# A linear-attention and mixture-of-experts layer on one core: feeding the routing block by block and moving slot lists, shared experts and routed experts between rounds

## The chip, the cores and the metric

The kernel runs on one NeuronCore of a Trainium2 chip. A core has TensorE (PE in the profile, with its weight loads as PEld), VectorE (DVE), ScalarE (ACT), GpSimd (POOL) and SyncE (SP), each with its own instruction stream in order, and 16 DMA engines that serve the queues of SP, ACT and POOL. The metric is the device time of one execution in microseconds (us). All data are float32.

## The reference

There are 4096 tokens (4 sequences of 1024) of 256 channels. The layer normalizes x and adds two branches to it: linear attention with 16 heads of 16 channels and four memory banks, and a mixture of 8 routed experts (two for each token, hidden size 176) with a shared expert of hidden size 352.

```python
xn = _layernorm(x, axis=-1)
x = x + _L0_attn_ref(xn, ...) + _L0_ffn_ref(xn, ...)
...
# attention
sq = elu1(q)
out_coarse = ...   # sq on the summed memory banks
out_fine = (outs * w).sum(0)          # sq on each bank, weighted
gprob = jax.nn.sigmoid(jax.nn.relu(coarse_repr @ eg_w1.T + eg_b1) @ eg_w2.T + eg_b2)
memory_output = exp_prob * out_fine + (1.0 - exp_prob) * out_coarse
local_output = causal_linear_attention(q, k, v)
gate = jax.nn.sigmoid(memory_gate).reshape(1, NH, 1, 1)
output = gate * memory_output + (1.0 - gate) * local_output
return output.transpose(0, 2, 1, 3).reshape(B, S, H) @ w_o.T
...
# experts
scores = jax.nn.softmax(logits, axis=-1)
topk_w, topk_idx = jax.lax.top_k(scores, K)
topk_w = topk_w / (jnp.sum(topk_w, axis=-1, keepdims=True) + 1e-20)
g = jax.nn.silu(jnp.einsum('th,efh->tef', x, w_gate)) * jnp.einsum('th,efh->tef', x, w_up)
expert_out = jnp.einsum('tef,ehf->teh', g, w_down)
y = jnp.einsum('te,teh->th', cw, expert_out).reshape(b, s, h)
y = y + _swiglu_mlp(x, sw_gate, sw_up, sw_down).reshape(b, s, h)
```

## The kernel before

A tile is 128 tokens, a block is 4 tiles; there are 32 tiles (`NTT`) and 8 blocks (`NBLK`). The order of the work is written out by hand: the Python program issues the instructions in the order in which each engine runs them, and waits between engines follow from the data and from the rotating buffers.

**Prelude.** SP's queue loads the eight blocks of x (`load_x`) and then all weights and constants except wvg, wq and wk, which are on ACT's queue. The string `ahead` gives the order of steps for each block: S (`statistics`: mean and variance of a row on DVE, then the power -0.5 on POOL for one or two blocks at once), N (`normalize`: half the tiles on DVE, half on ACT, in place, then SP's queue stores the block to `xns` in DRAM), T (`transpose_x`) and V (`values`: PE makes the values and the router's logits; ACT copies the values into the buffer that held x, and POOL sets their ones and zeros). The values overwrite the normalized x, so these writes wait for the store to `xns`. `masks`, `memories`, `gates`, `living` and `route` (the first and second largest logit, for half of the tokens) stand between them. After the prelude SP copies x to `sums` in DRAM, where the experts' results are added.

**Start.** The sorting of the tokens by expert (`route(1)`, `sort`, `weights`, `owners`; on DVE) runs beside the first query, key and shared-expert projections, among them the shared expert of block 0.

**Rounds.** Round n works on tile n in attention, with parts of tiles n-1 and n-2 (`attention_round`): scores, masks, memory, local part, the transposition back, the state update, and the output projection of tile n-2 (for tiles below 24). `quad`, four PSUM banks, holds the scores and then the memory products. All other PSUM results take turns in a pool of four banks (`bank`, tag r). Beside the attention round lie up to three further streams, which `mix` merges by the share of each stream's weight that is done:

- `lists`, in rounds 0 to 3 (`first_round` = 4): the slot lists that say which token stands in which slot of which expert. For each of 22 batches of three columns DVE makes one-hots (L540, L544; in buffers of the experts' weights), ACT and POOL weigh them (L557, L560), and PE adds them up in one bank, "found" (L568), which stays taken until the lists are done. `inverted` then gives `islot` and `wslot`.
- `beside`: shared expert of block 1 over rounds 0 to 3, then from round 4 for each block 2 to 7 over four rounds the keys of that block, the queries of the next one and (up to block 6) its shared expert (`projections`). The shared expert's hidden values stay in buffers with the tag h (2 x `NF` = 6 of 2 KB) until the output of their block.
- `side`, rounds 4 to 29: the routed experts, 71 tiles of slots (`NST`). `expert_turn` fetches rows of `xns` (an indirect DMA on POOL's queue, L1006) and weights (SP's queue), and transposes; `expert_hidden` (L1052, L1057 to L1059), `expert_out` (L1065, L1069), and `put`, an indirect DMA that adds the rows to `sums` (L1074). Each put waits for the one before it. A planner gives each round as many units as fill it up to a common level, at most 1.5 times the mean.

```python
    work = experts()
    share = [weight(rounds[n]) + weight(beside[n]) for n in range(first_round, last_round)]
    level = max(share)
    cap = 1.5 * weight(work) / len(share)
```

**Tail.** Round 30 has the shared expert of block 7. Then the outputs of tiles 24 to 31, which were held, run with rounds 31 to 33; `sums` is read back (L942, L978), added (L966, L992) and stored.

Of the kernel before, what the change touches and what calls it, by code (L numbers as in the profile page):

```python
# [8 lines left out]
FP = mybir.dt.float32  # L9
# [5 lines left out]
P = 128  # L15
# [7 lines left out]
def linear_attention_moe_kernel(  # L23
# [76 lines left out]
    def load_x(blk):  # L100

        wide = big.tile([P, NT, VW], FP, tag="tok", name=f"x_{blk}")
        xb = wide[:, :, :H]
        nc.sync.dma_start(
            xb, x[blk * TB : (blk + 1) * TB, :].rearrange("(n p) h -> p n h", p=P)
        )
        st["x", blk] = xb
        st["wide", blk] = wide

    for blk in range(NBLK):  # L110
        load_x(blk)

    def load_weight(w, name, engine=nc.sync):
        t = const.tile([P, NC, w.shape[1]], FP, tag=name, name=name)
        engine.dma_start(t, w.rearrange("(k p) c -> p k c", p=P))
        return t

    wvg = load_weight(w_vg, "wvg", nc.scalar)
    wq = load_weight(w_q, "wq", nc.scalar)
    wk = load_weight(w_k, "wk", nc.scalar)  # L120
    raw = const.tile([P, NC, NMN, D1], FP, tag="raw", name="raw")
    nc.sync.dma_start(
        raw[:, :, 1:NMN, :], memories.rearrange("(c p) m k -> p c m k", p=P)
    )
    gate = const.tile([P, NH], FP, tag="gate", name="gate")
    nc.sync.dma_start(gate, memory_gate.to_broadcast([P, NH]))
    b2 = const.tile([P, 1], FP, tag="b2", name="b2")
    nc.sync.dma_start(b2, eg_b2.to_broadcast([P, 1]))
    w1 = load_weight(eg_w1, "w1")
    b1 = const.tile([P, HID], FP, tag="b1", name="b1")  # L130
    nc.sync.dma_start(b1, eg_b1.rearrange("h o -> o h").to_broadcast([P, HID]))
    w2 = const.tile([P, HID], FP, tag="w2", name="w2")
    nc.sync.dma_start(w2, eg_w2.rearrange("h o -> o h").to_broadcast([P, HID]))
    wo = load_weight(w_o, "wo")
    wg = load_weight(w_gate[:, FR:], "wg")
    wu = load_weight(w_up[:, FR:], "wu")
    wd = const.tile([P, NF, H], FP, tag="wd", name="wd")
    full = FS // P
    nc.sync.dma_start(
        wd[:, :full, :],  # L140
        w_down[FR : FR + full * P, :].rearrange("(f p) h -> p f h", p=P),
    )
    if full < NF:
        nc.sync.dma_start(wd[: FS - full * P, full, :], w_down[FR + full * P :, :])

# [10 lines left out]
    nc.gpsimd.memset(ones, 1.0)  # L156
    neghalf = const.tile([P, 2 * NT], FP, tag="neghalf", name="neghalf")
    nc.gpsimd.memset(neghalf, -0.5)
# [46 lines left out]

    pick = tmp.tile([P, 2, NTT, E], FP, tag="h", name="pick", bufs=2 * NF)
    picks, pick = pick, [pick[:, r] for r in range(2)]
    lgs = tmp.tile([P, 2, NTT, E], FP, tag="h", name="lgs", bufs=2 * NF)
    lgs, gatew = lgs[:, 0], lgs[:, 1]

    more = tmp.tile([P, 2, E, NTT], FP, tag="h", name="more", bufs=2 * NF)[:, 0]
    nc.gpsimd.memset(more, 1.0)
# [16 lines left out]

    def sigmoid(v):  # L230

        nc.scalar.activation(v, v, AF.Exp, scale=-1.0)
        nc.vector.tensor_scalar(v, v, 1.0, None, ALU.add)
        nc.vector.reciprocal(v, v)

    def masks():
# [5 lines left out]
        for c in range(NC):  # L242
            nc.vector.tensor_copy(own_s[:, c], own[:, :, None].to_broadcast([P, HC, D1]))

    def gates_of_heads():
        nc.vector.tensor_scalar(gate, gate, -80.0, None, ALU.max)
        sigmoid(gate)
        nc.vector.tensor_scalar(ungate, gate, -1.0, 1.0, ALU.mult, ALU.add)
        nc.vector.tensor_copy(
            gates.rearrange("p (h k) -> p h k", k=HD), gate[:, :, None].to_broadcast([P, NH, HD])  # L250
        )
        nc.vector.tensor_scalar(b2, b2, 0.5, None, ALU.mult)
# [39 lines left out]

    def statistics(blk):

        xb = st["x", blk]
        if blk == 0 or blk % 2:
            st["mv"] = small.tile([P, 2, NT, 2], FP, tag="mv", name=f"mv_{blk}", bufs=3)
            st["rstd"] = small.tile([P, 2, NT], FP, tag="rstd", name=f"rstd_{blk}", bufs=3)
        mv, rstd = st["mv"], st["rstd"]
        at = (blk + 1) % 2 if blk else 0  # L300
        for i in range(NT):
            stats = small.tile([P, 6], FP, tag="stats", name=f"stats_{blk}_{i}")
            nc.vector.bn_stats(stats, xb[:, i, :])
            nc.vector.bn_aggr(mv[:, at, i, :], stats)
        st["norm", blk] = mv[:, at], rstd[:, at]
        if blk % 2 == 0 or blk == NBLK - 1:
            n = at + 1
            some = rstd[:, :n].rearrange("p b i -> p (b i)")
            nc.vector.tensor_scalar(
                some, mv[:, :n, :, 1].rearrange("p b i -> p (b i)"), LN_EPS, None, ALU.add  # L310
            )
            nc.gpsimd.tensor_tensor(some, some, neghalf[:, : n * NT], ALU.pow)

    def normalize(blk):

        xb = st["x", blk]
        mv, rstd = st.pop(("norm", blk))
        shift = small.tile([P, NT], FP, tag="shift", name=f"shift_{blk}")
        nc.vector.scalar_tensor_tensor(
            shift, mv[:, :, 0], -1.0, rstd, ALU.mult, ALU.mult  # L320
        )
        xnT = io.tile([P, NC, TB], FP, tag="xnT", name=f"xnT_{blk}")
        st["xnT", blk] = xnT
        half = NT // 2
        for i in range(half, NT):
            nc.vector.tensor_scalar(
                xb[:, i, :], xb[:, i, :], mv[:, i, 0:1], rstd[:, i : i + 1],
                ALU.subtract, ALU.mult,
            )
        for i in range(half):  # L330
            nc.scalar.activation(
                xb[:, i, :], xb[:, i, :], AF.Identity,
                bias=shift[:, i : i + 1], scale=rstd[:, i : i + 1],
            )
        nc.sync.dma_start(
            xns[blk * TB : (blk + 1) * TB, :].rearrange("(n p) h -> p n h", p=P), xb
        )

    def transpose_x(blk, pair):
# [81 lines left out]
    def weights():  # L421
# [7 lines left out]
        two = st["two"]  # L429
        both = tmp.tile([P, 2, NTT, E], FP, tag="h", name="chosen", bufs=2 * NF)  # L430
        yield
# [497 lines left out]
    def shared_hidden(blk, f):  # L929
        n = min(P, FS - f * P)  # L930
        th, pu = st.pop(("th", blk, f))
        h = tmp.tile([P, TB], FP, tag="h", name=f"h_{blk}_{f}", bufs=2 * NF)
        nc.vector.scalar_tensor_tensor(h[:n], th[:n], 0.5, pu[:n], ALU.mult, ALU.mult)
        st["h", blk, f] = h
# [147 lines left out]

    first_round, last_round = 4, 30

# [53 lines left out]
    def projections(blk):  # L1138

        pairs = keys(blk) + (queries(blk + 1) if blk + 1 < NBLK else [])  # L1140
        pairs += shared(blk) if blk + 1 < NBLK else []
        units = [u for pair in pairs for u in pair]
        if blk % BPB == 0:
            b = blk // BPB
            at = units.index(pairs[3][1]) + 1
            units[at:at] = [(64, mean_queries, b)]
            at = units.index(pairs[6][0])
            units[at:at] = [(64, batch_weights, b)]
# [22 lines left out]
    def experts():  # L1171
        units = [(2000, lambda: None), (256, expert_turn, -2), (256, expert_turn, -1)]
        for j in range(NST + 1):
# [7 lines left out]
    def split(units, parts):  # L1181
# [14 lines left out]

    ahead = "S0 S1 masks N0 T0 S2 S3 N1 N2 V0 T1 T2 S4 memories V1 S5 N3 N4 V2 T3 T4 S6 gates V3 S7"
    ahead += " N5 N6 V4 living T5 T6 N7 V5 route V6 T7 V7"
    other = {
        "masks": masks, "memories": memories_by_group, "gates": gates_of_heads, "living": living,  # L1200
        "route": lambda: [None for _ in route(0)],
    }
    with tc.tile_pool(name="ps_v", bufs=2, space=bass.MemoryType.PSUM) as ps_v:
        for what in ahead.split():
            if what in other:
                other[what]()
                continue
            blk = int(what[1:])
            if what[0] == "S":
                statistics(blk)  # L1210
            elif what[0] == "N":
                normalize(blk)
            else:
                for pair in range(NT // 2):
                    (transpose_x if what[0] == "T" else values)(blk, pair)

# [22 lines left out]

    rounds = [attention_round(n) for n in range(NTT + 2)]  # L1240
    beside = [[u for pair in shared(1) for u in pair if u]] + [projections(blk) for blk in range(2, NBLK)]
    beside = [units for run_of in beside for units in split(run_of, NT)] + [[]] * (NT + 2)
    lists = []
# [20 lines left out]
    level = max(share)  # L1264
    cap = 1.5 * weight(work) / len(share)
    while sum(min(cap, max(0, level - s)) for s in share) < weight(work):
# [80 lines left out]
```

## Time and profile before

| | us |
|---|---|
| median of 3 runs (lowest, highest) | 720.52 (717.43, 724.11) |
| the profiled execution, its own time | 720.73 |
| its span, first to last instruction | 718.8 |
| PE busy in the span | 656.1 (91%) |
| DVE busy | 455.8 (63%) |
| POOL busy | 385.6 (54%) |
| ACT busy | 266.9 (37%) |

The profile comes from one execution. "Busy" of an engine is the time in which at least one of its instructions ran; matmuls are pipelined, so a busy PE isn't at its peak. A row of a timeline gives the start, the time taken, the engine, the line of the kernel, the operation, what it writes and reads, its size, how many instructions are merged, and in square brackets how long the engine stood idle before it and what ended that. A row of the windows view gives for a stretch of time the busy time of each engine with the number of instructions, the clock granted to PE (1.00 is full), the share of the DMA engines' time, and GB/s.

Rounds are found in the trace by their first matmuls, the scores (L691): round 0 starts at 88.7 us, round 4 at 165.2, round 26 at 583.4, round 30 at 671.7.

### The profile page before, as it was taken

Reading aid. Unit: us, or ns where it says so; the run is one execution under the profiler, and the core shown is the slowest. Engines: PE = TensorE matmul, PEld = TensorE weight load, DVE = VectorE, ACT = ScalarE, POOL = GpSimd, SP = SyncE. Lnnn points to the kernel's source line nnn. Section 1 sums busy time; section 2 is a strip of 40 time slices with the busy share of each in tenths; the row PEclk is TensorE's granted clock in tenths of the full one; section 3 lists DMA queues with packets and bytes.
Section 4 is the critical chain, followed back from the end, with each engine's and each line's share of the span. In section 5 each row is a group of like instructions: output and inputs, shape, how many; then the busy total and the mean of one; then the engine's idle time right before and its main releaser. Section 6 shows DMA issues by size and latency. Waiting matters only on the chain.

```text
span 718.8 us, 14242 instructions
## 1 busy us (share of the span) xinstructions
PE 656.1 (91%) x5084; PEld 468.4 (65%) x5084; DVE 455.8 (63%) x1193; ACT 266.9 (37%) x614; POOL 385.6 (54%) x436
## 2 busy tenths in 40 slices
PE   3699987888999999999999999999999987998987
PEld 2585465675676667766676766676767765665666
DVE  6544888886675656665756665657656654454764
ACT  3365443333433343334333442344333433243310
POOL 3210034455465566565664564646665777666576
PEclk9899988999999999999999999999999999699999
DMA  9556000014344444443444453535445676575285
GB/s 295 175 189 190 1 1 1 1 29 115 86 108 102 111 98 89 103 119 86 115 108 91 108 107 77 123 91 116 111 96 123 136 182 145 123 157 126 30 269 206
DMA packets 86466, 81.50 MB, mean 113 GB/s; under 512 B 7533, under 2 KB 83997, under 8 KB 86269
## 3 DMA queue, kind: packets, MB, share of 16 engines
q1 hardware_dynamic: 70797, 60.14, 29.1%
q0 software_dynamic: 13632, 18.62, 15.2%
q10 hardware_dynamic: 1968, 1.84, 0.7%
q8 instruction: 40, 0.66, 0.4%
q14 instruction: 29, 0.24, 0.1%
HBM read 62.62 MB, written 22.15 MB: 118 GB/s over the span
## 4 chain that ended last, share of the span: by engine, by line
PE 71%; DMA 9%; DVE 8%; POOL 4%; ACT 4%; issue 3%; SPq 0%; ACTq 0%; POOLq 0%; DVEq 0%
PE phe L1052 11%; PE pye L1065 7%; PE psu L921 6%; PE po L958 6%; PE pg L907 5%; DMA sums<-y,islot 4%; PE quad L691 4%; PE pn L717 4%; PE po L962 4%; PE quad L806 3%; PE pk L600 3%; PE pq L600 3%; PE pv L362 2%; PE pte L1039 2%; PE pte L1043 2%
## 5 line engine op out<-in xcount | busy, mean ns | idle before, releaser
L1074 POOL DMA_INDIRECT sums<-y,islot x71 | 113.3, 1595 | 80.0 <-DMA sums<-y,islot 28.4
L1052 PE MATMUL phe<-wgu,turned 128*128 128x352 f32 x276 | 99.5, 484 | 2.5 <-ACT turned L1045 1.2
L1058 DVE SCALAR_TENSOR_TENSOR hidden<-hidden,phe 128x176 f32<-128x176 f32 x71 | 23.8, 335 | 117.8 <-ACT hidden L1057 113.2
L698 DVE TENSOR_TENSOR sT<-quad,causal 128x512 f32<-128x512 f32 x128 | 80.6, 681 | 8.1 <-PE quad L691 7.8
L1006 POOL DMA_INDIRECT xg<-xns,islot x71 | 70.3, 990 | 19.7 <-issue 10.6
L1065 PE MATMUL pye<-wdn,turned 88*128 88x256 f32 x284 | 77.3, 395 | 1.8 <-issue 1.4
L828 POOL TENSOR_TENSOR cg<-coarse,gates 128x256 f32<-128x256 f32 x32 | 24.5, 767 | 98.0 <-DVE h L885 53.5
L1052 PEld LDWEIGHTS phe<-wgu,turned 128*128 128x128 f32 x276 | 49.5, 195 | 27.0 <-issue 8.3
L1065 PEld LDWEIGHTS pye<-wdn,turned 88*128 88x128 f32 x284 | 51.2, 194 | 15.3 <-issue 6.7
L1069 ACT ACTIVATE y<-pye,wslot 128x256 f32<-128x256 f32 x71 | 33.6, 473 | 70.8 <-PE pye L1065 59.0
L1045 ACT COPY turned<-pte 128x512 f32<-128x512 f32 (+1 forms) x71 | 41.0, 578 | 46.7 <-PE pte L1043 43.1
L846 POOL TENSOR_TENSOR fm<-fm 128x512 f32<-128x512 f32 x32 | 44.0, 1374 | 26.7 <-DVE prob L894 16.6
L1057 ACT ACTIVATE hidden<-phe 128x176 f32<-128x176 f32 x71 | 22.5, 317 | 71.3 <-PE phe L1052 67.6
L958 PE MATMUL po<-wd,h 128*128 128x256 f32 (+1 forms) x192 | 47.4, 383 | 0.1
L907 PE MATMUL pg<-xnT,wg 128*128 128x512 f32 (+1 forms) x96 | 47.4, 617 | 0.0
L921 PE MATMUL psu<-xnT,wu 128*128 128x512 f32 (+1 forms) x96 | 47.0, 613 | 0.2 <-DVE skT L618 0.2
L835 DVE TENSOR_TENSOR fm<-quad,rw 128x512 f32<-128x512 f32 x64 | 41.9, 680 | 0.0
L560 POOL TENSOR_TENSOR held<-ones,two 128x213 f32<-128x213 f32 (+1 forms) x22 | 16.0, 736 | 44.9 <-DVE ones L540 44.9
L896 DVE SCALAR_TENSOR_TENSOR o<-diff,prob,loc 128x256 f32<-128x256 f32 x32 | 37.4, 1167 | 3.4
L362 PE MATMUL pv<-wvg,xnT 128*128 128x264 f32 x128 | 32.9, 418 | 7.0 <-ACT xnT L347 7.0
L958 PEld LDWEIGHTS po<-wd,h 128*128 128x128 f32 (+1 forms) x192 | 34.9, 190 | 6.4 <-issue 0.4
L806 PE MATMUL quad<-mem,sqT 32*128 32x170 f32 x512 | 28.9, 341 | 7.6 <-DVE sT L698 7.5
(210 smaller groups left out, 1376.1 us busy)
## 6 DMA issues: line engine op xcount, KB each, us to landing
wgu<-in_w_gate_dram SPq DMA_DIRECT2D x71, 176.0 KB
wgu<-in_w_up_dram SPq DMA_DIRECT2D x71, 176.0 KB
wdn<-in_w_down_dram SPq DMA_DIRECT2D x71, 176.0 KB
x<-in_x_dram SPq DMA_DIRECT2D x8, 512.0 KB
xns<-x SPq DMA_DIRECT2D x8, 512.0 KB
sums<-in_x_dram SPq DMA_DIRECT2D x8, 512.0 KB
part<-sums SPq DMA_DIRECT2D x12, 256.0 KB
out_dram<-acc SPq DMA_DIRECT2D x12, 256.0 KB
```

The costliest lines, as they stand in the source:

```text
L362: nc.tensor.matmul(pv[:, j, : H + E], xnT[:, k, i * P : (i + 1) * P], wvg[:, k, :], start=(k == 0), stop=(k == NC - 1),)
L600: nc.tensor.matmul(pq, w[:, k, c * P : (c + 1) * P], xnT[:, k, :], start=(k == 0), stop=(k == NC - 1),)
L698: nc.vector.tensor_mul(sT, quad[:, g, :].rearrange("p (c t) -> p c t", t=P), causal[:, None, :].to_broadcast([P, NC * 2, P]),)
L806: nc.tensor.matmul(quad[:, g, c * KM : (c + 1) * KM], sqT[rows, c, tok], mem[rows, c, :], start=True, stop=True,)
L846: nc.gpsimd.tensor_add(fm[:, :, 0:2, :], fm[:, :, 0:2, :], fm[:, :, 2:4, :])
L907: nc.tensor.matmul(pg[:n, :], wg[:, k, f * P : f * P + n], xnT[:, k, :], start=(k == 0), stop=(k == NC - 1),)
L921: nc.tensor.matmul(pu[:n, :], wu[:, k, f * P : f * P + n], xnT[:, k, :], start=(k == 0), stop=(k == NC - 1),)
L958: nc.tensor.matmul(po[:, :H], st["h", blk, f][:k, tok], wd[:k, f, :], start=(f == 0), stop=False)
L1006: nc.gpsimd.indirect_dma_start(out=xg, out_offset=None, in_=xns, in_offset=bass.IndirectOffsetOnAxis(ap=islot[:, j : j + 1], axis=0),)
L1052: nc.tensor.matmul(ph[:, : 2 * F], xgT[:, k, :], wgu[:, k].rearrange("p g f -> p (g f)"), start=(k == 0), stop=(k == NC - 1),)
L1065: nc.tensor.matmul(py[:, :H], hT[:FH, f, :], wdn[:, f, :], start=(f == 0), stop=(f == 1))
L1074: nc.gpsimd.indirect_dma_start(out=sums, out_offset=bass.IndirectOffsetOnAxis(ap=islot[:, j : j + 1], axis=0), in_=st.pop(("y", j)), in_of ...
```

## The change

- x of block 0 is loaded in two halves, the second on ACT's queue. Of the weights only wvg is loaded at once; every other load waits in a list, `loads`, in a new order, and `normalize` issues two of them on SP's queue after each store to `xns`.
- `statistics` works on half a block at a time, and the power on POOL is taken for each block alone. `ahead` has a new order in which the values of block n lie between the steps of blocks n+1 and n+2. The exponential of the gates (`exps`) is parted from the rest of their sigmoid.
- `first_round` is 2: the slot lists run in rounds 0 and 1, the experts from round 2 to 29. Rounds 0 and 1 have the whole shared experts of blocks 1 and 2 beside them, rounds 2 and 3 none. The shared expert of block 6 moves from rounds 20 to 23 to rounds 26 to 29. In the blocks that have only keys and queries the queries come first.
- The planner's cap is 1.25 times the mean in place of 1.5, and the first, empty unit of the experts weighs 3000 in place of 2000.
- Tag h has 3 x `NF` = 9 buffers.

```diff
         xb = wide[:, :, :H]
-        nc.sync.dma_start(
-            xb, x[blk * TB : (blk + 1) * TB, :].rearrange("(n p) h -> p n h", p=P)
-        )
+        parts = 2 if blk == 0 else 1
+        n = NT // parts
+        for part in range(parts):
+            rows = slice((blk * NT + part * n) * P, (blk * NT + (part + 1) * n) * P)
+            (nc.scalar if part else nc.sync).dma_start(
+                xb[:, part * n : (part + 1) * n],
+                x[rows, :].rearrange("(n p) h -> p n h", p=P),
+            )
...
+    loads = []
+
+    def load_weight(w, name, engine=None):
+        t = const.tile([P, NC, w.shape[1]], FP, tag=name, name=name)
+        src = w.rearrange("(k p) c -> p k c", p=P)
+        if engine is None:
+            loads.append(lambda: nc.sync.dma_start(t, src))
+        else:
+            engine.dma_start(t, src)
+        return t
+
+    load_x(0)
+    wvg = load_weight(w_vg, "wvg", nc.scalar)
+    for blk in range(1, NBLK):
         load_x(blk)
...
+    wq = load_weight(w_q, "wq")
+    wk = load_weight(w_k, "wk")
...
-    def statistics(blk):
+    def statistics(blk, half):
...
+        n = NT // 2
+        for i in range(half * n, (half + 1) * n):
             stats = small.tile([P, 6], FP, tag="stats", name=f"stats_{blk}_{i}")
             nc.vector.bn_stats(stats, xb[:, i, :])
...
+        if half:
+            nc.vector.tensor_scalar(rstd, mv[:, :, 1], LN_EPS, None, ALU.add)
+            nc.gpsimd.tensor_tensor(rstd, rstd, neghalf, ALU.pow)
...
             xns[blk * TB : (blk + 1) * TB, :].rearrange("(n p) h -> p n h", p=P), xb
         )
+        for _ in range(2):
+            if loads:
+                loads.pop(0)()
...
-        h = tmp.tile([P, TB], FP, tag="h", name=f"h_{blk}_{f}", bufs=2 * NF)
+        h = tmp.tile([P, TB], FP, tag="h", name=f"h_{blk}_{f}", bufs=3 * NF)
...
-    first_round, last_round = 4, 30
+    first_round, last_round = 2, 30
...
-        pairs += shared(blk) if blk + 1 < NBLK else []
+
+        pairs += shared(blk) if 2 < blk < NBLK - 2 else []
+        if len(pairs) == 4:
+            pairs = pairs[2:] + pairs[:2]
...
-        units = [(2000, lambda: None), (256, expert_turn, -2), (256, expert_turn, -1)]
+        units = [(3000, lambda: None), (256, expert_turn, -2), (256, expert_turn, -1)]
...
-    ahead = "S0 S1 masks N0 T0 S2 S3 N1 N2 V0 T1 T2 S4 memories V1 S5 N3 N4 V2 T3 T4 S6 gates V3 S7"
-    ahead += " N5 N6 V4 living T5 T6 N7 V5 route V6 T7 V7"
+    ahead = "S0a S0b S1a N0 T0 S1b S2a N1 V0a T1 V0b S2b S3a N2 V1a T2 V1b masks S3b S4a N3 V2a T3 V2b"
+    ahead += " memories S4b S5a N4 V3a T4 V3b living S5b S6a N5 V4a T5 V4b route exps S6b S7a N6 V5a T6"
+    ahead += " V5b S7b N7 V6a T7 V6b gates V7a V7b"
...
-    beside = [[u for pair in shared(1) for u in pair if u]] + [projections(blk) for blk in range(2, NBLK)]
-    beside = [units for run_of in beside for units in split(run_of, NT)] + [[]] * (NT + 2)
+    beside = [[u for pair in shared(blk) for u in pair if u] for blk in (1, 2)] + [[], []]
+    for blk in range(2, NBLK):
+        beside += split(projections(blk), NT)
+    beside += [[]] * (NT + 2)
+    late_shared = split([u for pair in shared(NBLK - 2) for u in pair if u], NT)
+    for n, units in zip(range(last_round - NT, last_round), late_shared):
+        beside[n] = beside[n] + units
...
-    cap = 1.5 * weight(work) / len(share)
+    cap = 1.25 * weight(work) / len(share)
```

## The prediction

> **What bounds the kernel now.** I read the page first (busy shares, the 40 slices), then the span cut into its stages, then the timelines of PE, ACT, DVE and POOL where PE is idle. In the page, 40 slices of 18 us:
>
> ```profile
> PE   3699987888999999999999999999999987998987
> PEclk9899988999999999999999999999999999699999
> DMA  9556000014344444443444453535445676575285
> ```
>
> PE is at 9 nearly everywhere. It is low in three places: the first two slices, slices 6 to 9 (0-based 5 to 8), and from slice 33 on, where PEclk also drops to 6. Cut at the first matmul of the query projections (59), of round 0 (88.7), 4 (165.2), 26 (583.4) and 30 (671.7); the columns are PE, weight loads, DVE, ACT, POOL, granted clock, DMA share, GB/s:
>
> ```profile
> 0.00:59.00 59.00, 40.73 (x196) 34.58 (x197) 29.40 (x133) 27.26 (x64) 13.39 (x68) 0.94 0.70 227
> 59.00:88.70 29.70, 29.35 (x77) 12.93 (x75) 23.88 (x66) 14.06 (x25) 0.00 (x0) 1.00 0.20 63
> 88.70:165.20 76.50, 61.15 (x571) 47.46 (x570) 63.02 (x140) 27.77 (x89) 35.41 (x45) 0.89 0.06 15
> 165.20:583.40 418.20, 408.42 (x3330) 288.64 (x3328) 264.71 (x676) 159.35 (x346) 244.69 (x238) 1.00 0.46 106
> 583.40:671.70 88.30, 77.39 (x613) 55.96 (x611) 46.57 (x118) 30.90 (x73) 61.42 (x57) 0.90 0.62 135
> 671.70:718.80 47.10, 39.10 (x311) 28.85 (x310) 28.24 (x62) 7.56 (x19) 30.72 (x30) 0.97 0.59 187
> ```
>
> PE is the bound in 165 to 583 (98% busy, full clock). Work taken from there is worth its PE price, and work put where PE idles costs little. PE idles 18.3 us in the prelude, 15.4 in rounds 0 to 3, 10.9 in rounds 26 to 29 and 8.0 in the tail; and in the third and fifth stage the clock is 0.89 and 0.90. Why the prelude idles (timelines of SP's queue, ACT, PE):
>
> ```profile
> 19.09 30.03 SPq L335 DMA_DIRECT2D xns<-x  x8
> 25.26 0.59 ACT L367 COPY x<-pv 128x512 f32<-128x512 f32 x1 [7.43 <-DMA xns<-x]
> 27.03 8.95 PE L362 MATMUL pv<-wvg,xnT 128*128 128x264 f32 x32 [6.66 <-ACT xnT L347]
> ```
>
> The values overwrite x, so ACT waits for block 0's store to xns. That store was issued at 19.09, after eleven loads of weights and constants on SP, and landed at 25.2; PE stood 6.66 us behind it. In rounds 0 to 3 (PE, then DVE):
>
> ```profile
> 91.82 0.81 PE L691 MATMUL quad<-sqT,skO 32*128 32x128 f32 x8 [2.66 <-ACT skO L678]
> 95.68 3.27 PE L907 MATMUL pg<-xnT,wg 128*128 128x512 f32 x4
> 153.74 1.88 PE L921 MATMUL psu<-xnT,wu 128*96 128x512 f32 x4
> 95.30 0.55 DVE L544 TENSOR_TENSOR ones<-count,lohi 128x384 f32<-128x384 f32 x1
> 108.07 1.08 DVE L544 TENSOR_TENSOR ones<-count,lohi 128x384 f32<-128x384 f32 x1
> ```
>
> After a gap of 2.66 us the same shape of group takes 3.27 in place of 1.88. DVE is as busy as PE here, and its one-hot doubles in time at some places. In rounds 26 to 29 (POOL, then PE):
>
> ```profile
> 576.03 1.59 POOL L1074 DMA_INDIRECT sums<-y,islot  x1 [1.64 <-DMA sums<-y,islot]
> 581.31 1.61 POOL L1074 DMA_INDIRECT sums<-y,islot  x1 [1.11 <-ACT hidden L1057]
> 611.35 0.69 PE L1043 MATMUL pte<-ident,xg 128*128 128x128 f32 x2 [3.69 <-DMA xg<-xns,islot]
> 612.68 2.55 PE L1052 MATMUL phe<-wgu,turned 128*128 128x352 f32 x4
> ```
>
> Each accumulating write of expert rows (put) waits for the one before it. From 566.85 to 682.76 there are 22 starts, so 21 intervals of 5.5 us. POOL is in order, so the row fetches, cg, fm, loc and state updates stand behind a waiting put; PE then waits 3.69 us for a fetch, and runs at half clock after it.
>
> **The change, stage by stage.** Prices are start to start at full clock in the PE timeline. A shared-expert matmul group is 1.72 us (six to a block: 10.3), a slot-list group (L568) 0.74, an expert 2.5 (1.19 + 0.87 + 0.43). An attention round is 4.8 without output, 7.5 with it (scores 1.1, turns 0.4, keys 0.44 in even rounds, memory 0.79, gate 0.39, local 1.01, back 0.9, update 0.5, output 2.17). I counted the planner's units from the text of both kernels. Slot lists go from rounds 0-3 into 0-1; shared(1) and shared(2) fill rounds 0 and 1, one block each; rounds 2-3 get 5 experts; rounds 4-25 keep 55 experts and lose shared(2) and shared(6); rounds 26-29 go from 16 experts to 11, plus shared(6).
>
> *Prelude, 59 to 54.* x of block 0 is halved over two queues, statistics become one block ahead, and all of SP's weight loads but none of ACT's wvg go behind the xns stores, two after each; wq and wk leave ACT's queue for SP's. In front of the first store only 4.2 MB of x and 0.27 of wvg remain. At the 370 GB/s that the DMA view shows from about 2.5 us on, with 0.5 MB of the store itself, it lands at about 16.5. V0's copy then runs some 8 us earlier. PE's block costs 3.65 (values) + 0.95 (transposes) = 4.6: after the first release seven values and six transposes remain, 31.2 us. With the release reaching PE at 18.5 and 2 to 4 us for the alternation N, V, T (ACT now works for one block at a time; N waits for POOL's pow, which stands behind the memsets that wait for the store) it ends at 52 to 54. I take 54; bounds 50 and 59 (the store is no longer early, if x's eight loads fill the queue). Moved loads: at most 1.26 us of SP each; wq, behind the second store, is wanted at 54 and should land before 25, wd, behind the sixth, only in round 2. Should that cover go, the first projection would wait for it at its landing. The copies of x to sums stay behind the last store on SP and move earlier with it; their reader is the first put, after 140.
>
> *At nothing:* eight pow of 1.05 for five of 1.05 to 1.65 (+1.3 on POOL, 13.4 busy of 59); exp of the gates split from its reciprocal, which takes away a DVE wait of 7.6 that only ACT's backlog made; masks later (first read in the rounds); three more 2 KB buffers for h (no instruction); queries before keys in blocks 2, 6 and 7 (batch weights, under 3 us of DVE, end a round that has DVE to spare).
>
> *Rounds 0-3, 76.5 to 96.* Rounds 0-1: PE 12 x 1.72 + 22 x 0.74 + 9.7 = 46.6. DVE: one-hots 28.7 (as measured, all slots), two rounds' own 16.6 (7.4 and 9.2), shared 12 x 0.67 = 8.1, together 53.4. DVE now ends last; at 0.87 busy (here it had 0.82 with less to mix) 61. Rounds 2-3: PE 15 + 5 x 2.5 = 27.5, times 1.07 (418 us of stage four against 390 from these prices) 29.4, and 5 for the start of the experts, whose first fetch needs the finished list (PE idled 3.00 there before, and no projection lies beside it now): 35. Sum 96.
>
> The clock is a place where row and rule differ. TensorE: Matmul & The Clock Gate, under "Why this matters for your kernels", has the clock fall only after idle gaps over about 3 us. Here 2.66 us was enough, while a gap of 3.00 at 161 us cost nothing. By the rule, closing gaps of 1.6 to 2.7 us wins only the gaps, and some 5 us of slow clock stay in rounds 0-1 (66, not 61). I take the row: shared(1) now precedes scores(0) in PE's order and fills that gap.
>
> A rule speaks against the change: SBUF — State Buffer, "SBUF: two separate sides", calls the port pair of DVE and GpSimd an exclusive lock, where the later of two two-input operations blocks. The trace agrees: a pair of one-hots costs 0.37 + 0.55 alone, and 0.90 + 1.11 at the dearest, beside POOL's held multiply (0.76). By the row's mean (1.30 a batch) DVE has 28.7; if in the denser mix every batch is blocked, 44.2. I keep the mean, since each batch still has one multiply, and keep 20.2 and 44.2 for the range.
>
> *Rounds 4-25, 418.2 to 397.6:* minus two shared blocks, 20.6. There are 3 experts a round in rounds 3-7 and 20-22, puts of 5.5 us against 18 of PE: rounds 24-25 held 7 experts before with PE full. Bounds 392 and 406.
>
> *Rounds 26-29, 88.3 to 70.* PE before: 21.4 + 16 x 2.5 + 1.7 = 63, but 18 puts in the plan x 4.9 = 88. Now PE has 21.4 + 27.5 + 10.3 + 1.7 = 61, times 1.07 = 65; puts 14 x 4.9 = 69. I take 70; bounds 64 and 88.
>
> *Start and tail* stay at 29.7 and 47.1: the last put is again the last expert's, and the sums' reload follows it.
>
> Sum: 54 + 29.7 + 96 + 397.6 + 70 + 47.1 = 694.4, against the profiled span of 718.8. With the 1.9 us that lie around it (that execution took 720.73) 696. The median shown is 720.52, the same within 0.2, so 696 stands for it too.
>
> **The rivals.** (a) *DVE blocked by the port:* all 22 batches at 2.01: DVE 68.9 / 0.94 = 73 in rounds 0-1, +12: 708. For it: the doubled one-hots; against: half the pairs were not blocked. (b) *The puts still set the end:* POOL's order with its shared work keeps 6.3 us a put, 14 of them again 88: 714. For it: single intervals of up to 7.3 us, and the 28.4 us of POOL's waits on the put before; against: rounds 24-25. (c) *Slower, by PSUM banks in rounds 0-1.* Four banks serve all; "found" holds one for both rounds, and 12 shared groups each want two turns of the three left (24), freed only by DVE, whose in-order queue has one-hot batches between. If every turn makes PE wait behind one batch, between the mean 1.33 and the dear 2.01, say 1.67, that is 40 us: 736. It makes the change slower than the bound of 1% from 1.3 us a turn. For it: the shared groups' density goes up fourfold there; against: in rounds 0-3 the waits view puts PE's waits on the held multiply (9.6), skO (2.7), masks (1.8), nT and held (1.3), which is all 15.4 of its idle time, and none on such a release, with the same list running. (d) *It doesn't do what it says* in the prelude: 59 stays, 701, inside the main case.
>
> **How the numbers follow.** Under about 1% (7.2 us) a measurement of this kernel can't be told from no change. Main case with (d) 0.58, 684 to 708; (a) 0.11; (b) 0.13; (c) 0.18. Faster is main and (a), 0.69; same is (b), 0.13; slower (c), 0.18. The range runs from the main case's low end, 684, over (a) and (b) with a few us of spread, to 721; (c) is left out.
>
> **What would show it.** The ACT copy of V0 starts near 17, not 25.26; query projections start near 54; round 2 starts near 145 in the new time (54 + 29.7 + 61), with DVE over 0.85 before it and PEclk at 1.0; round 26 to 30 takes some 70 with no wait of PE on xg above 2 us. PE waits on a DVE release of bank r in rounds 0-1, of 1 us and more and many times, would show (c); one-hot means at 0.9 and 1.1 (a). I am wrong if rounds 4-25 don't give back the two shared blocks, which says that PE wasn't their bound.

## The result, and the profile after

The changed kernel takes 714.0 us (median of 7 runs, 710.40 to 716.88) where the kernel before takes 722.87 in the same session (7 runs, 717.43 to 726.43). The ratio is 0.9885, 95% interval 0.9856 to 0.9914: 8 us faster, a third of the 24 that were forecast. The profiled execution took 711.61 with a span of 709.9, against 718.8 before. The 40 slices of its page, now 17.7 us each:

```profile
PE   4897979989999989999999999999898998898986
PEclk9999999999999999999999999999999999999999
```

The prelude (slices 0 to 2) is denser, the low slices of the early rounds are down to two (5 and 8), and no slice has a low clock. But slice 3, where the start begins, is at 7, and there are 8s from slice 28 on, late in the rounds. The same stages as before, cut at the first matmul of the query projections (54.0), at the end of the start's last matmul (88.9), and at rounds 2, 4, 26 and 30 (columns as in the table of before: us, busy time of PE, weight loads, DVE, ACT and POOL with their instructions, granted clock, DMA share, GB/s):

```profile
0.00:54.00 54.00, 41.33 (x197) 34.00 (x198) 30.76 (x136) 27.39 (x64) 14.57 (x71) 0.97 0.72 227
54.00:88.90 34.90, 30.87 (x73) 13.44 (x71) 23.92 (x65) 13.69 (x25) 0.00 (x0) 0.95 0.28 86
88.90:144.80 55.90, 50.09 (x376) 34.18 (x375) 44.62 (x107) 24.93 (x81) 25.74 (x33) 0.97 0.06 16
144.80:178.40 33.60, 30.20 (x293) 23.13 (x292) 22.24 (x56) 12.03 (x27) 20.07 (x21) 1.00 0.51 131
178.40:580.40 402.00, 389.67 (x3273) 282.24 (x3272) 259.29 (x658) 155.17 (x338) 249.30 (x240) 0.99 0.49 110
580.40:661.90 81.50, 71.09 (x579) 48.86 (x578) 45.55 (x118) 26.89 (x63) 51.39 (x50) 0.96 0.45 98
661.90:709.90 48.00, 40.04 (x311) 30.09 (x310) 25.21 (x60) 6.94 (x17) 26.86 (x27) 0.93 0.58 181
```

| stage | before | forecast | after | after less forecast |
|---|---|---|---|---|
| prelude | 59.0 | 54 | 54.0 | 0 |
| start | 29.7 | 29.7 | 34.9 | +5.2 |
| rounds 0-1 / 2-3 (76.5 together before) | | 61 / 35 | 55.9 / 33.6 | -5.1 / -1.4 |
| rounds 4-25 | 418.2 | 397.6 | 402.0 | +4.4 |
| rounds 26-29 | 88.3 | 70 | 81.5 | +11.5 |
| tail | 47.1 | 47.1 | 48.0 | +0.9 |
| span | 718.8 | 694.4 | 709.9 | +15.5 |

So three stages owe time of note (the start, rounds 4 to 25 and above all rounds 26 to 29), and one (rounds 0-1) gives 5 us more than forecast.

**The prelude's 5 us come and go.** ACT's first copy of values, and PE's first query projection, in the timelines of after:

```profile
17.57 0.59 ACT L389 COPY x<-pv 128x512 f32<-128x512 f32 x1 [4.80 <-DMA xns<-x]
53.99 5.31 PE L622 MATMUL pq<-xnT,wq 128*128 128x512 f32 x12
```

V0's copy is 7.7 us earlier than before, the projections start 5 us earlier. Twelve microseconds on (SP's queue, then ACT and PE):

```profile
49.80 3.79 SPq L1250 DMA_DIRECT2D sums<-in_x_dram  x6
53.70 0.51 SPq L1251 DMA_DIRECT2D sums<-zero  x1
55.11 0.34 SPq L1252 DMA_DIRECT2D xns<-zero  x1
65.84 0.60 ACT L627 ACTIVATE eq<-pq 128x512 f32<-128x512 f32 x1 [6.96 <-DMA xns<-zero]
67.89 3.13 PE L622 MATMUL pk<-xnT,wk 128*128 128x512 f32 x4 [3.92 <-DVE sqT L636]
```

The wait for the same store before:

```profile
66.72 0.60 ACT L605 ACTIVATE eq<-pq 128x512 f32<-128x512 f32 x1 [2.82 <-DMA xns<-zero]
```

The third `eq` of the queries takes the buffer that held `zero` (tag "wide", three buffers). `zero` is stored to the last rows of `sums` and `xns`, and SP issues these two stores behind the eight copies of x to `sums`, 4 MB read and 4 MB written. The last one is issued at 55.1 and lands at 65.8. Before, it landed at 66.7, and ACT, which came later, lost 2.8 us to it. The landing has hardly moved, so ACT, 5 us earlier now, waits 6.96, and PE 3.92 behind it.

**Rounds 26 to 29 wait for the masks.** PE's largest waits there before, and the largest after, in the waits view (us in total, times, longest):

```profile
PE pte L1043 <- DMA xg<-xns,islot: 6.3, 4, 3.7
PE quad L806 <- DVE sT L698: 3.2, 3, 1.5
```

```profile
PE quad L828 <- DVE sT L720: 7.9, 4, 2.4
```

The first of the four after, in the timelines of DVE and PE:

```profile
585.40 0.60 PE L790 MATMUL pk<-ident,skT 128*128 128x128 f32 x4
586.08 0.34 DVE L1080 SCALAR_TENSOR_TENSOR hidden<-hidden,phe 128x176 f32<-128x176 f32 x1 [2.82 <-ACT hidden L1079]
586.70 1.28 DVE L720 TENSOR_TENSOR sT<-quad,causal 128x512 f32<-128x512 f32 x2
588.04 0.86 PE L828 MATMUL quad<-mem,sqT 32*128 32x170 f32 x16 [2.04 <-DVE sT L720]
588.83 1.98 PE L929 MATMUL pg<-xnT,wg 128*128 128x512 f32 x4
```

DVE runs in order. Two of the masks stand behind an expert's `hidden`, which waits 2.82 us for PE's product and ACT's tanh. The memory products need the masks, since they overwrite the scores in `quad`. Up to round 25 an output projection (2.17 us of PE) lies between masks and memory; from round 26 on it is held for the tail, and what is left there (for this wait, down to the product `pk` at 585.40) ends before the masks do. The shared-expert group that the change brings (L929) stands behind the memory, where it covers nothing. Before, the outputs of these rounds were held too, and the same wait was 3.2 us; 6.3 more went to late row fetches (`xg`), which no longer appear among PE's waits. That the masks are late because of `hidden` is read from this row; no run puts them ahead of it.

**In rounds 4 to 25** PE waits 4.6 us for odd keys, nearly all of it at rounds 8 and 24, the first rounds after blocks 2 and 6 have been projected with queries ahead of keys:

```profile
PE quad L713 <- ACT skO L700: 4.6, 4, 2.3
```

**The two costs that were feared are absent.** PE's waits in rounds 0-1 are 3.6 and 2.1 us on weighted one-hots (`held`) and none on a free bank. The one-hots in that stage, by form (busy us, mean ns, idle before):

```profile
L566 DVE TENSOR_TENSOR ones<-count,lohi 128x384 f32<-128x384 f32 x21 | 13.1, 624 | 0.0
L562 DVE TENSOR_TENSOR ones<-count,lohi 128x213 f32<-128x213 f32 x21 | 10.0, 475 | 5.3 <-issue 3.3 <-PE found L590 1.9
```

A pair costs 1.10 in the mean, where the same view before has 1.33 (16.3 and 11.7 us for 21 pairs), and rival (a) had 2.01. What lengthens a one-hot is also not quite what the forecast took it for. Of the 44 one-hots before, 14 took 0.75 us or more, and 11 of these ran beside POOL's own work for the attention round (`cg`, `diff`, `loc`, `state`), 3 beside the batch's multiply (`held`) alone. After there are 5 such, all beside the round's work; the dearest pair, 1.23 + 1.07 us from 113.06 on, ran beside `fm` and `diff`. The same 22 batches now meet the work of two rounds and not of four. That fits the lower mean; no run tests it.

### The profile page after: what moved, and what is told of

Read it like the earlier page. It is cut to its first block, busy times and chain, and to the rows that moved or that the text cites. A ratio compares the mean times of both kernels' runs of the same rounds, so it can differ in the third digit from the quotient of the medians.

```text
span 709.9 us, 14253 instructions
## 1 busy us (share of the span) xinstructions
PE 653.3 (92%) x5084; PEld 465.9 (66%) x5084; DVE 451.6 (64%) x1196; ACT 267.0 (38%) x614; POOL 387.9 (55%) x439
## 4 chain that ended last, share of the span: by engine, by line
PE 78%; DVE 10%; DMA 4%; ACT 4%; issue 2%; POOL 1%; SPq 1%; DVEq 0%; ACTq 0%; POOLq 0%
PE phe L1074 12%; PE pye L1087 9%; PE po L980 6%; PE psu L943 6%; PE pg L929 5%; PE quad L713 5%; PE pk L622 4%; PE pn L739 4%; PE po L984 4%; PE quad L828 4%; PE pq L622 3%; PE pte L1061 2%; PE found L590 2%; PE pv L384 2%; PE pte L1065 2%
## 5 line engine op out<-in xcount | busy, mean ns | idle before, releaser
L1074 PE MATMUL phe<-wgu,turned 128*128 128x352 f32 x276 | 97.6, 476 | 3.7 <-issue 2.3
L1087 PEld LDWEIGHTS pye<-wdn,turned 88*128 88x128 f32 x284 | 49.6, 189 | 17.0 <-issue 10.9
L1091 ACT ACTIVATE y<-pye,wslot 128x256 f32<-128x256 f32 x71 | 33.6, 473 | 70.4 <-PE pye L1087 70.3
L929 PE MATMUL pg<-xnT,wg 128*128 128x512 f32 (+1 forms) x96 | 47.7, 621 | 0.1
L828 PE MATMUL quad<-mem,sqT 32*128 32x170 f32 x512 | 28.2, 335 | 10.3 <-DVE sT L720 10.3
L838 DVE TENSOR_SCALAR rw<-quad 128x80 f32<-128x80 f32 x32 | 7.6, 238 | 45.0 <-PE quad L828 45.0
L918 DVE SCALAR_TENSOR_TENSOR o<-diff,prob,loc 128x256 f32<-128x256 f32 x32 | 33.3, 1042 | 3.6
```

The costliest lines, as they stand in the source:

```text
L828: nc.tensor.matmul(quad[:, g, c * KM : (c + 1) * KM], sqT[rows, c, tok], mem[rows, c, :], start=True, stop=True,)
L929: nc.tensor.matmul(pg[:n, :], wg[:, k, f * P : f * P + n], xnT[:, k, :], start=(k == 0), stop=(k == NC - 1),)
L1074: nc.tensor.matmul(ph[:, : 2 * F], xgT[:, k, :], wgu[:, k].rearrange("p g f -> p (g f)"), start=(k == 0), stop=(k == NC - 1),)
L1087: nc.tensor.matmul(py[:, :H], hT[:FH, f, :], wdn[:, f, :], start=(f == 0), stop=(f == 1))
```

## The experiments

The theory after this reading had three parts: (A) rounds 26 to 29 lack cover behind the masks; (B) the start loses the prelude's gain to the zeros' store; (C) the queries-first order costs the odd keys' wait. The chief rival for A is that puts still set the pace, as the forecast's rival (b) had it: its 714 us is what came out, and its 6.3 us a put also agrees (13 puts start from 585.01 to 661.01 in the trace). Ratios are to the kernel before on the same chip.

**Prelude alone** (kernel before with the new loads, `statistics`, `normalize` and order):

```diff
-    ahead = "S0 S1 masks N0 T0 S2 S3 N1 N2 V0 T1 T2 S4 memories V1 S5 N3 N4 V2 T3 T4 S6 gates V3 S7"
+    ahead = "S0a S0b S1a N0 T0 S1b S2a N1 V0a T1 V0b S2b S3a N2 V1a T2 V1b masks S3b S4a N3 V2a T3 V2b"
...
```

> The kernel before with the changed prelude alone (x of block 0 in two halves, loads behind the stores, half-block statistics, the new order of steps). Theory of the sum: the first query projection starts at 54 us in place of 59 and nothing behind it changes, so 5 us less than before, a ratio of 0.993. Rival, gain lost later: the sorting or the sums copies take it back, ratio 0.998 or more.

0.9994 (0.9969 to 1.0019). The projections start at 55.70, against 59.0 before; then ACT waits 6.74 us on `zero`, PE 3.69 behind it, and round 0 starts at 89.27 against 88.66 before. The gain is there at 56 us and gone at 89, as the rival had it.

**Rounds alone** (the change with the old prelude):

```diff
-    first_round, last_round = 4, 30
+    first_round, last_round = 2, 30
...
-    cap = 1.5 * weight(work) / len(share)
+    cap = 1.25 * weight(work) / len(share)
```

> The change without its prelude (old loads, statistics and order of steps, new rounds and planner). If the parts add up, it is the 8.9 us of the two profiles less the prelude's 5, so about 4 us less than before, a ratio of 0.9945; rounds 26 to 29 again near 81 us. Rival: the parts hang together (a late prelude delays the lists), ratio 1.0.

0.9893 (0.9854 to 0.9933), the gain of the whole change. The 0.9945 that was expected took off 5 us for the prelude, which by the run above gives nothing.

**Cover for the masks** (A): the late shared-expert units are placed between masks and memory, in place of being spread over the round.

```diff
-        beside[n] = beside[n] + units
+        k = next(i for i, u in enumerate(rounds[n]) if u[1] is memory)
+        rounds[n] = rounds[n][:k] + units + rounds[n][k:]
```

> The change with the late shared expert's units of rounds 26 to 29 set between the masks and the memory products in place of being spread over the round. Theory A (PE waits for the masks, because the output projection that lay between scores and memory is missing in these rounds): PE's wait on the masks in rounds 26 to 29 falls from 7.9 to under 3 us, its clock stays at 1.0, the stretch shrinks from 81.5 to 72 to 75, and the whole is 7 us shorter than the change, ratio to before 0.979. Theory B (the chain of puts still sets these rounds): the stretch stays at 79 or more.

0.9717 (0.9689 to 0.9745), 704.15 us. Rounds 26 to 29 in the windows view, and PE's largest wait in them:

```profile
584.70:656.20 71.50, 67.33 (x581) 46.84 (x580) 49.94 (x118) 26.81 (x63) 49.67 (x49) 1.00 0.50 112
```

```profile
PE pu L808 <- DVE loc L773: 1.3, 1, 1.3
```

The wait for masks is gone, and the stage takes 71.5, near the 70 of the forecast; the whole gains more than the 7 us expected. Of the 10 us in the stage, 3.8 are PE's busy time for the same matmuls (67.33 for 71.09): the clock is at 1.00 rather than 0.96. That part can't be counted on, as the next run shows.

**Two sums** (the puts): odd tiles' results are added to a second tensor, so that neighbouring puts don't wait for each other. Nobody reads that tensor, so the output lacks these results.

```diff
+    sums2 = dram.tile([T + P, H], FP, tag="sums2", name="sums2")
...
-            out=sums,
+            out=sums2 if j % 2 else sums,
```

> The change with the odd expert tiles added to a second tensor in DRAM that nobody reads, so that a put no longer waits for the one just before it; the results of half of the expert tiles are left out of the output. Theory A (masks): rounds 26 to 29 within 3 us of 81.5. Theory B (puts): POOL's wait on the put before is gone and the stretch shrinks to 74 or less, the whole by 7 us or more.

0.9826 (0.9786 to 0.9866). Waits of a put on the one before are gone (0.3 us are left), and neighbours start as little as 1.89 us apart (641.72 and 643.61). PE's largest wait and the stage:

```profile
PE quad L829 <- DVE sT L721: 7.9, 4, 2.3
```

```profile
580.25:658.44 78.19, 67.78 (x578) 46.92 (x577) 44.83 (x114) 26.85 (x63) 49.36 (x47) 1.00 0.45 101
```

The masks' wait is untouched. The stage is 3.3 us shorter, just outside the 3 us that theory A allowed and far from the 74 of theory B. These 3.3 us are the clock, not the puts: a later run ("keys first, with the batch weights behind the scores") has the change's own late rounds, with the puts chained, and there

```profile
580.60:658.80 78.20, 67.79 (x580) 47.00 (x579) 46.22 (x118) 26.85 (x63) 51.36 (x50) 1.00 0.45 102
```

So at full clock these rounds take 78.2 us with chained puts and without, and the puts are not their bound; 6.3 us a put was the pace of the rounds that the puts followed. That rival had the right number for the wrong reason. The cover's sure part is 78.2 to 71.5, 6.7 us; the rest hangs on whether the clock falls after the gaps.

**Zeros first** (B): in the change, and in the kernel with the new prelude alone.

```diff
+    nc.sync.dma_start(sums[T:, :], zero[:, :H])
+    nc.sync.dma_start(xns[T:, :], zero[:, :H])
     for blk in range(NBLK):
         rows = slice(blk * TB, (blk + 1) * TB)
         nc.sync.dma_start(sums[rows, :], x[rows, :])
-    nc.sync.dma_start(sums[T:, :], zero[:, :H])
-    nc.sync.dma_start(xns[T:, :], zero[:, :H])
```

> The change with the two stores of zeros issued on SP's queue before the eight copies of x to sums. Theory: ACT's 6.96 us wait in the start (its third exponential takes the buffer of the zeros, whose store lands only behind the copies) is what gave the prelude's 5 us back; without it the start is 30 us in place of 34.9 and the whole about 4 to 5 us shorter than the change, ratio 0.982. Rival (the sorting on DVE is as late in any case): the start stays at 33 or more.

> The kernel before with the changed prelude alone (as in e1) and the zeros' stores first. Theory: now the prelude's gain shows, 5 us and up to 2.8 more for the wait that the kernel before had itself: ratio 0.990 to 0.993, against 0.999 of e1. Rival: the gain is lost further on, at the first rounds, whatever the zeros do: 0.998 or more.

In the change the ratio is 0.9838 (0.9799 to 0.9877); with the prelude alone 0.9928 (0.9903 to 0.9953), where it was 0.9994 without this edit, and round 0 starts at 83.31 in place of 89.27. The start of the changed kernel with zeros first:

```profile
54.00:83.20 29.20, 29.09 (x75) 13.06 (x73) 23.79 (x65) 14.08 (x25) 0.00 (x0) 1.00 0.35 110
```

PE has no idle time left in it, and its clock is at 1.00. B holds. In the change the median is 0.0047 lower, but the intervals overlap; the pair with the prelude alone is the clearer one.

**Keys first** (C):

```diff
-        if len(pairs) == 4:
-            pairs = pairs[2:] + pairs[:2]
...
-            at = units.index(pairs[3 if len(pairs) > 6 else 1][1]) + 1
+            at = units.index(pairs[3][1]) + 1
```

> The change with the keys before the queries again in blocks 2 and 6. Theory: PE's waits on skO at the start of rounds 8 and 24 (1.89 and 2.31 us) come from keys that are projected last before the round that needs them; they fall under 0.5 and rounds 4 to 25 take 398 in place of 402, ratio 0.983. Rival: the waits only move to the batch weights or the queries, no difference beyond 1 us.

0.9944 (0.9923 to 0.9966), slower than the change. The odd keys' wait is down to 0.4 us, but the batch weights now come right behind the mean of the queries that they need, and PE, in order, waits for it (waits view of this run, rounds 4 to 25):

```profile
PE pr L662 <- DVE qr L651: 9.4, 2, 5.2
```

9.4 us for 4.6, and rounds 4 to 25 take 412.5 us in this profile, where 398 was expected: the order in the change is the cheaper of the two, and C as stated falls. Covers, zeros and keys together, with the edits above:

> The change with the shared units between masks and memory (e3), the zeros first and the keys first. If the three faults lie at different places they add up: 704.15 less 5 less 4, about 695 to 697, ratio 0.962. If one covers another: 700 or more.

0.9759 (0.9722 to 0.9795), behind the cover alone, as the keys' price is in it.

**Cover and zeros without keys:**

> The changed kernel with the two edits that helped alone: the held-back shared expert of block 6 put between the masks and the memory of rounds 26 to 29, and the zeros stored ahead of the copies of x to sums; queries stay before keys. If the start and the late rounds are separate losses, the gains add: the first alone stood at 0.9717 of the kernel before, the second took 0.0047 off the change's 0.9885, so 0.967, about 699 us. If the 5 us of the earlier start only run into the puts or the tail once the rounds are dense, it is no better than 0.9717.

0.9686 (0.9643 to 0.9729), where the theory had 0.967; the interval doesn't exclude 0.9717.

**Another cover** (A again): block 6's outputs are not held, and its shared expert is in rounds 20 to 23 as before the change.

```diff
-    held_from = NTT - 2 * NT
+    held_from = NTT - NT
...
-        pairs += shared(blk) if 2 < blk < NBLK - 2 else []
+        pairs += shared(blk) if 2 < blk < NBLK - 1 else []
...
-    for n, units in zip(range(last_round - NT, last_round), late_shared):
-        beside[n] = beside[n] + units
```

> The changed kernel with another cover in the same place: the output projections of block 6 are not held for the tail but run in rounds 26 to 29 between masks and memory, as in all rounds before, and the shared expert of block 6 goes back into rounds 20 to 23. If what rounds 26 to 29 lack is any work of TensorE behind the masks, the waits for the masks there fall from 7.9 us each to about nothing and the clock stays up, the four projections (8.7 us) leave the tail for those rounds, and the whole is near 0.974 (about 704 us). If it is the shared expert's own instructions or the puts that hold the rounds up, it stays at 0.985 or above.

**Block 6's shared expert back, nothing in its place** (the second and third hunk of that edit alone):

> The changed kernel with block 6's shared expert back in rounds 20 to 23, and nothing in its place. My theory: held back where nothing pins it behind the masks it covers little, so bringing it back changes little: 0.985 to 0.993 of the kernel before, and the waits for the masks in rounds 26 to 29 stay. A rival, that holding it back is what keeps the expert tiles from crowding into the last rounds, gives 0.995 or more; another, that it is pure loss there, gives 0.98 or less.

The first is at 0.9702 (0.9675 to 0.9729), the second at 0.9770 (0.9741 to 0.9799). Their rounds 26 to 29, in this order:

```profile
584.10:655.20 71.10, 69.02 (x605) 52.41 (x604) 44.96 (x110) 27.76 (x63) 51.44 (x49) 0.98 0.55 124
```

```profile
585.00:656.50 71.50, 63.33 (x569) 46.06 (x568) 45.08 (x113) 26.68 (x63) 50.94 (x48) 0.95 0.55 122
```

With outputs as cover no wait for a mask is left (7.9 us in total in the change, not each), and the tail falls from 48.0 to 45.0. With nothing in its place, 4.9 us of waits for masks stay, and yet the stage takes 71.5, 10.0 less than in the change (81.5, at clocks of 0.95 and 0.96). So behind the waits the shared groups cost at least their price on PE (six groups of 1.72, 10.3), the more so as the planner puts 12 experts into these rounds here and not 11 (48 matmuls of `phe` for 44). In rounds 4 to 25 the same groups add only 4.0 (406.0 for 402.0). The one expert that has left that stage is an estimated 2.5 us of the difference, by the forecast's price. I had expected 0.985 to 0.993; the rival that holding back is pure loss where nothing pins it was right. Another part may be that block 6 is then projected keys first, with the shared groups between the queries' mean and the next round: the odd keys' wait fell from 4.6 to 3.1 us here and to 1.0 with the outputs as cover.

**The cap alone:**

```diff
-    cap = 1.25 * weight(work) / len(share)
+    cap = 1.5 * weight(work) / len(share)
```

> The changed kernel with the cap on one round's share of the expert tiles at 1.5 of the mean again in place of 1.25. By the planner's weights the cap binds only in rounds 2, 3, 25, 27 and 29, and one or two tiles move. If the even spread is worth nothing by itself, the ratio stays at 0.985 to 0.992; if it is what eases the puts, it is above 0.993, with waits of POOL or TensorE for the rows and puts in the late rounds.

0.9855 (0.9822 to 0.9888): the more even spread is worth nothing that these runs can tell. The weight of 3000 and the nine buffers of tag h were not run alone.

**Keys first, with the batch weights behind the scores of rounds 8 and 24** (C, mended):

```diff
-            at = units.index(pairs[6][0]) if len(pairs) > 6 else len(units)
-            units[at:at] = [(64, batch_weights, b)]
+            if len(pairs) > 6:
+                at = units.index(pairs[6][0])
+                units[at:at] = [(64, batch_weights, b)]
...
+    for b in (1, 3):
+        rounds[b * BPB * NT][1:1] = [(64, batch_weights, b)]
```

> The changed kernel with keys ahead of queries in blocks 2 and 6, as in the run before that came out slower, but with the batch weights behind the scores of round 8 and of round 24 in place of the last unit before them. My theory: the swap in the change is there for the mean of the queries, on which the batch weights wait, and the odd keys' wait (4.6 us in rounds 4 to 25) is its price; with the weights moved neither wait is left, so 4 to 5 us less than the change: 0.980 to 0.984. A rival, that TensorE's order of work in rounds 7 and 23 is what cost 5 us in that run and the wait for the mean only shows it, gives 0.992 or more again.

0.9841 (0.9798 to 0.9884). PE's wait on the mean is down from 9.4 to 0.9:

```profile
PE pr L662 <- DVE qr L651: 0.9, 1, 0.9
```

So the place of the batch weights was the 5 us of "keys first". But rounds 4 to 25 take 402.7 here against 402.0 in the change: the odd keys' wait went, and a new one of 2.2 us (`pte` on the experts' `hidden`) and the 0.9 came, with 1.6 us more of PE's busy time (391.2 for 389.7). The lower median is not told from the change's.

**Outputs as cover, with zeros first, and then with keys first in block 2 too** (the edits above):

> The output projections of block 6 as the cover of rounds 26 to 29, block 6's shared expert back in rounds 20 to 23, and the zeros stored ahead of the copies of x to sums. The first two stood at 0.9702; if the start's loss is a separate one, 5 us less again: 0.963, about 696 us. If the earlier start is eaten by later waits, 0.970.

> The kernel of the run above with keys ahead of queries in block 2 and its batch weights behind the scores of round 8 (block 6 has its shared expert again and so keeps keys first by itself). By my theory one wait for odd keys less, some 2 us: 0.960. By the rival it is 0.966 or more.

0.9642 (0.9599 to 0.9685), 696.26 us, and 0.9638 (0.9592 to 0.9683), 695.77 us. Round 4 starts at 173.7 us in the first, where it starts at 179.8 with the same cover and without the zeros (0.9702), and the end keeps it: spans of 693.3 and 700.2. So with this cover the losses A and B add. The keys' order shows nothing again: 0.9638 lies between the 0.960 of the theory and the 0.966 of its rival. Both beat both kernels.

## Why the prediction was right or wrong

The direction was right, the size was not. By its steps:

- **Prelude, "59 to 54": right.** The store's landing sets V0's copy (17.57; "near 17"), and the projections start at 53.99.
- **"Start and tail stay at 29.7 and 47.1": the start failed,** 34.9. The forecast checked who reads what the moved copies write ("the first put, after 140"), and not who stands behind them in SP's queue. Two small stores did, and a buffer's next user waited for those. The prelude alone and zeros first, with and without the rounds, show it. The tail, 48.0, held.
- **Rounds 0-3, "96": mis-sized in the good direction,** 89.5. The forecast had DVE end last in rounds 0-1, over 0.85 busy with 53.4 us; it had 44.6 of 55.9 (0.80), and PE, with 50.1 (0.90), was the busier. The one-hots are 4.9 of the 8.8 us (21 pairs took 23.1, and 28.0 before). The 2.01 of rival (a) added the dearest of each form; no pair before took more than 1.98. Rivals (a) and (c) did not come. That round 2 starts at 144.77, "near 145", is luck: the start lost 5.2 us and rounds 0-1 gained 5.1. On the clock the row (a gap of 2.66 us slows) stood nearer than the rule of the Trainium skill that the forecast set against it (TensorE: Matmul & The Clock Gate, "Why this matters for your kernels": gaps over about 3 us): waits of 1.7 to 2.4 us were followed by a slow clock in the late rounds, though not each time. What it meant for rounds 0-1 can't be told, as the new order leaves a gap of 3.58 us there.
- **Rounds 4-25, "397.6": 402.0.** The two shared blocks were given back for the most part (16.2 of 20.6), so PE is the bound there. "Queries before keys" stood at nothing and has a wait of 4.6 us. Whether that wait is the missing 4.4 is not settled: without it other waits came, and the stage was no shorter.
- **Rounds 26-29, PE at "61, times 1.07 = 65", puts at 69, "I take 70": the step that failed,** 81.5. The factor 1.07 came from rounds 4 to 25, whose masks are covered by the output projection; here there is none, and the sum of PE's work says nothing of what lies behind which wait. The relief of the puts came as forecast (no late fetch on PE), but a wait for masks took its place: 8.2 of the 11.5 us at full clock (78.2), and 3.3 for the clock that fell behind two of the four waits in this execution. With a cover the stage is 68.3 to 72.5 over six profiles. The term of the puts stood on weak readings too: from 566.85 to 682.76 there are 23 starts before, so intervals of 5.27, and in rounds 26 to 29 before 16 puts start (88.3 us, 5.5 each), not the 18 of the plan at 4.9. At 5.5, 14 puts would have been 77. As the puts were not the bound, this isn't what failed.

Of the 15.5 us by which the span missed, the late rounds are 11.5 and the start 5.2, both shown by their removal (the price of the late rounds but for the part that hangs on the clock): with both mended the kernel takes 696.26, where the forecast had 696. That the figures meet is in part chance, since other edits (block 6's shared expert back, its outputs out of the tail) are in that run, and rounds 0-1 had been overestimated.

## What to carry to other kernels

When work is moved into a stretch, ask what it will stand in front of on its in-order engine: here matmuls placed behind a wait cost their whole price (10.3 us), and the same ones placed in it won back 6.7 us of it at full clock. A factor of overhead taken from one stage holds only where the same cover is there. When a transfer moves, list what is queued behind it and which buffers those wait to free, however small they are.

## What the runs showed of the hardware

- A store of 128 KB issued at 55.1 us landed at 65.8: 10.7 us, behind 4 MB of copies from DRAM to DRAM on the same queue. Issued ahead of them, nobody waited for it.
- Whether the clock falls after a gap of 1.7 to 2.4 us isn't fixed. With the same four waits for masks (1.74, 1.75, 2.04 and 2.35 us) the late rounds had clocks of 1.00, 0.96 and 0.94 in three profiles, and took 78.2, 81.5 and 83.2 us. A fall shows in single rows: after the same 2.04 us the same four matmuls (`pg`) took 1.98 us in one and 3.14 in another.
- An accumulating put that waited for the one before it (2.83 us) started 4.4 us behind it (642.73 and 647.13 in the run with cover; 4.5 to 5.1 in the late rounds of the change). To two tensors in turn, two starts were as close as 1.89 us, with 1.6 us of POOL each.
